# Routed results of a mixture of experts: through a buffer, or added to the stored output rows by the scatters

## The chip, the cores and the metric

The kernel runs on one core of one Trainium2 chip. The metric is the device time of one execution in microseconds, where less is better. The profile is one execution recorded by the hardware profiler; its span runs from the first to the last instruction on the core, and its times are counted from the start of that span. Engines are called PE (matrix products; its weight loads have rows of their own, PEld), DVE (vector engine), ACT (scalar engine), POOL or GpSimd, and SP, which here only issues DMAs. The DMAs that move rows to places given by an index tensor ("indirect") are issued by GpSimd.

## The reference

One layer of three parts over 512 tokens (8 sequences of 64) of width 512, all in float32: three rounds of slot attention over contexts of 1601 rows, a self-attention with 16 heads, and a mixture of experts. Each part normalises its input and adds its result to x. Only the third matters here:

```python
logits = xf @ router_w + router_b                      # 512 tokens x 8 experts
topk_vals, topk_idx = jax.lax.top_k(logits, 2)
gates = softmax over the two chosen, 0 elsewhere
expert(x, w1, w3, w2) = (silu(x @ w1) * (x @ w3)) @ w2  # 512 -> 256 -> 512
routed_out = sum over the 8 experts of gate * expert(xf)
shared_out = expert_s0(xf) + expert_s1(xf)              # two experts that every token passes
return x + routed_out + shared_out
```

So each output row is the sum of the row of x, two shared results and two routed results.

## The kernel before, in words

The first two parts, and the norm in front of the third, fill the span up to about 844 us and are untouched. `xall` (line 125) holds the 512 rows of x as four tiles of 128 rows in on-chip memory; every part adds its result into it.

The third part goes as follows.

- *Routing* (lines 973 to 1055). DVE finds each token's two experts and gates. Rows that go to the same expert are packed into blocks of 128 rows; an expert's last block is padded. There are at least 8 and at most `NB` = 15 blocks; `NB_MOST` = 12 are always computed, the other three only under a condition (line 1147) that this run does not meet.
- *Rows out to the blocks* (lines 1057 to 1066). Eight indirect DMAs write each token's normalised row twice into `xbuf` in device memory, at its place in its block. A row in `xbuf` is `DX` = 514 wide: 512 values, then the row number to which its result goes (column `D`, an integer), then its gate (column `D + 1`). `xbuf` was first filled with zero rows whose row number is one past the last legal one (lines 899 to 905), so that padding rows are skipped by the bounds check of the later scatter. In the old kernel the row number is a place in `back`, which has one row for each token and choice: 1024 rows.
- *Shared experts*. `shared_up(e, tp, ...)` (line 850) computes the first two products and the gate of shared expert `e` for the token pair-tile `tp` (256 tokens); `shared_down` (line 868) does the last product, 8 matmuls in the trace's counting (rows `py_s`, line 875), and adds it into `xall` on DVE (line 880). There are four such combinations. (0,0) runs during the routing, (0,1) in front of the blocks. For (1,0) and (1,1) only `shared_up` runs in front of the blocks; their `shared_down` is kept in the list `later`.
- *Blocks*. `block_up(n)` (line 1084) issues on GpSimd's queue the load of the block's 128 rows from `xbuf` into an `xb` buffer (six of them), reads the block's expert number into a register on SP, and loads that expert's weights on SP's queue (`up_b`, `dn_b`; `up_b` has five buffers, tag `ctxT`). PE transposes the rows (`tr_xb`), DVE or ACT copies them out, PE multiplies (`pab`), ACT and DVE apply the gate function (`th`, `g`). `block_down(n)` (line 1102) transposes `g`, does the second product (`py`), ACT scales it by the gates into `y` (three buffers, line 1114), and GpSimd scatters the 128 rows of `y` with an indirect DMA (line 1115), taking the row numbers straight from `xb`. Program order is up of block n+1, then down of block n. The scatters are declared independent of each other (line 1122) because they write distinct rows.
- *The end* (lines 1149 to 1166). The two late `shared_down` run, and for each of the four row tiles `back`'s two results for a token are loaded by SP behind all scatters, added to `xall` (by DVE alone, or after GpSimd has added the two), and stored to `out` by a DMA on ACT's queue.

`queue` (line 127) issues a DMA on SP in the written order; `behind(inst, those)` (line 1068) makes an instruction wait for others. What is not tied by such a call or by `keep_in_program_order` may be placed by the scheduler in an order of its own within an engine's queue; each engine then works through its queue strictly in order, so an instruction that waits holds up all behind it.

Of the kernel before, what the change touches and what calls it, by code (L numbers as in the profile page):

```python
# [9 lines left out]
F32 = mybir.dt.float32  # L10
I32 = mybir.dt.int32
AF = mybir.ActivationFunctionType
ALU = mybir.AluOpType
AX = mybir.AxisListType

P = 128
D = 512
DC = D // P
B, S = 8, 64
NPAIR = B * S // P  # L20
# [7 lines left out]
TOP = 2  # L28
DX = D + 2
NB_MOST = 12  # L30
# [10 lines left out]
def perceiver_kernel(  # L41
# [7 lines left out]
    nc = tc.nc  # L49
# [5 lines left out]
    dram = ctx.enter_context(  # L55
        tc.tile_pool(name="dram", bufs=1, space=bass.MemoryType.DRAM)
    )
# [10 lines left out]
    def chunk(name, tag="w"):  # L68

        bufs, width = SLOTS[tag]  # L70
        return big.tile([P, width], F32, tag=tag, name=name, bufs=bufs)
# [4 lines left out]
    def bank(name, tag="ring"):  # L76
        return ps.tile([P, 512], F32, tag=tag, name=name)
# [47 lines left out]
    xall = const.tile([P, NPAIR, D], F32, name="xall")  # L125

    def queue(dst, src):

        return tc.keep_in_program_order(nc.sync.dma_start(dst, src))  # L129
# [32 lines left out]
    def matmul4(dst, lhsT, rhs, start=True, stop=True):  # L162
        for c in range(DC):
            last = nc.tensor.matmul(  # L164
                dst, lhsT=lhsT(c), rhs=rhs(c),
                start=start and c == 0, stop=stop and c == DC - 1,
            )
        return last
# [55 lines left out]
    places, tag_of = [], {}  # L224
# [306 lines left out]
    def recur_more(t, banks, c):  # L531

        for j, k in ((2, DC - 1), (1, c))[c > 0 :]:
            tc.keep_in_program_order(nc.tensor.matmul(  # L534
                banks[j], lhsT=sT_of[t][:, k, :], rhs=whh_s[j][:, k, :],
                start=k == 0, stop=j == 2,
            ))
# [109 lines left out]
    for pos, (half, (t, it)) in enumerate(stages[:-1]):  # L647
# [21 lines left out]
        if it == 0:  # L669
# [14 lines left out]
            t, it, fill=lambda c: recur_more(other[0], begun[other], c)  # L684
# [159 lines left out]
    def gated(dst, th, pa, pb):  # L844

        nc.scalar.activation(th, pa, AF.Tanh, scale=0.5)
        nc.vector.scalar_tensor_tensor(th, th, 1.0, pa, ALU.add, ALU.mult)
        nc.vector.scalar_tensor_tensor(dst, th, 0.5, pb, ALU.mult, ALU.mult)

    def shared_up(e, tp, tags):  # L850

        up = shared[e][0]
        n = f"s{e}_{tp}"
        cols = ts(tp, 2 * P)
        g = chunk(f"g_{n}", tags[1])[:, :D] if tags[1] in SLOTS else work.tile(
            [P, D], F32, tag=tags[1], name=f"g_{n}", bufs=3
        )
        g = g.rearrange("p (c m) -> p c m", c=HC)
        for hc in range(HC):
            pab = bank(f"pab_{n}_{hc}")  # L860
            pa, pb = pab[:, : 2 * P], pab[:, 2 * P :]
            matmul4(pa, lambda c: up[:, c, ts(hc, P)], lambda c: hT[:, c, cols])
            matmul4(pb, lambda c: up[:, c, ts(HC + hc, P)], lambda c: hT[:, c, cols])
            th = work.tile([P, D], F32, tag=tags[0], name=f"th_{n}_{hc}")[:, : 2 * P]
            gated(g[:, hc, :], th, pa, pb)
        return g

    def shared_down(e, tp, g, at=lambda add: add()):

        dn = shared[e][1]  # L870
        for h in range(2):
            t = 2 * tp + h
            py = bank(f"py_s{e}_{tp}_{h}")
            for hc in range(HC):
                nc.tensor.matmul(  # L875
                    py, lhsT=g[:, hc, ts(h, P)], rhs=dn[:, hc, :],
                    start=hc == 0, stop=hc == HC - 1,
                )
            at(lambda t=t, py=py: tc.keep_in_program_order(
                nc.vector.tensor_add(xall[:, t, :], py, xall[:, t, :])  # L880
            ))
# [13 lines left out]


    xbuf = dram.tile([NB * P, DX], F32, name="xbuf")
    back = dram.tile([TOP * NPAIR * P, D], F32, name="back")
    zeros = chunk("zeros")[:, :DX]
    nc.gpsimd.memset(zeros, 0.0)  # L900
    nc.gpsimd.memset(zeros[:, D : D + 1].bitcast(I32), TOP * NPAIR * P)
    tc.keep_in_program_order(nc.gpsimd.dma_start(
        xbuf.rearrange("(b p) d -> p b d", p=P),
        zeros.unsqueeze(1).to_broadcast([P, NB, DX]),
# [3 lines left out]
    for i in range(TOP):  # L908
        rows = chunk(f"rows_{i}")[:, : NPAIR * DX].rearrange("p (t d) -> p t d", d=DX)
        nc.gpsimd.iota(  # L910
            rows[:, :, D].bitcast(I32), pattern=[[P, NPAIR]], base=i * NPAIR * P,
            channel_multiplier=1,
        )
        rows_of.append(rows)
# [8 lines left out]
    def part_of(*shape):  # L923
        n = shape[0] * shape[-1] if len(shape) > 1 else shape[0]
        lo = taken[0]
        taken[0] += n
        v = room[:, lo : lo + n]
        return v.rearrange("p (t e) -> p t e", e=shape[-1]) if len(shape) > 1 else v

    before, every, numbers = part_of(P), part_of(P), part_of(NB)  # L930
    rank, base = part_of(NPAIR, E), part_of(NPAIR, E)
# [4 lines left out]
        out=before, in_=before, compare_op=ALU.is_ge, fill=0.0, base=-1,  # L936
        pattern=[[1, P]], channel_multiplier=-1,
# [72 lines left out]
    blocks = sums[0][:, E:]  # L1010
# [46 lines left out]
    for t in range(NPAIR):  # L1057
        for i in range(TOP):
            at = bass.IndirectOffsetOnAxis(ap=place[i][:, t : t + 1], axis=0)
            s = nc.gpsimd.indirect_dma_start(  # L1060
                out=xbuf[:], out_offset=at, in_=rows_of[i][:, t, :], in_offset=None
            )
# [5 lines left out]
    def behind(inst, those, reason="rows of the blocks"):  # L1068
        for s in those:
            tc.add_manual_dep(  # L1070
                inst.ins, s.ins.name,
                mybir.DependencyInfo(
                    mybir.DependencyClass.Sync, mybir.DependencyReason.DATA
                ),
                reason=reason,
            )
# [25 lines left out]
    def block_down(n, xb, g, dn):  # L1102
        pt = bank(f"tr_g_{n}")[:, :HF].rearrange("p (c m) -> p c m", c=HC)
        for c in range(HC):
            nc.tensor.transpose(pt[:, c, :], g[:, ts(c, P)], ident)
        gT = work.tile([P, HC, P], F32, tag="gT", name=f"gT_{n}", bufs=2)
        nc.vector.tensor_copy(gT, pt)
        py = bank(f"py_{n}", "gate")
        for c in range(HC):
            nc.tensor.matmul(  # L1110
                py, lhsT=gT[:, c, :], rhs=dn[:, c, :], start=c == 0, stop=c == HC - 1
            )
        y = work.tile([P, D], F32, tag="y", name=f"y_{n}", bufs=3)
        nc.scalar.mul(y, py, xb[:, D + 1 :])
        s = nc.gpsimd.indirect_dma_start(
            out=back[:], in_=y, in_offset=None,
            out_offset=bass.IndirectOffsetOnAxis(ap=xb[:, D : D + 1].bitcast(I32), axis=0),
            bounds_check=TOP * NPAIR * P - 1, oob_is_err=False,
        )
        if n < NB_MOST:  # L1120
            if returned:
                tc.declare_no_dep(s.ins, group="returned", reason="rows of distinct places")
            tc.add_to_no_dep_group("returned", s.ins)
            returned.append(s)

    returned = []
    later = []
    for e, tp in ((0, 1), (1, 0), (1, 1)):
        later.append((e, tp, shared_up(e, tp, ("th", "g"))))
        if e == 0:  # L1130
            shared_down(*later.pop())

    def run_blocks(lo, hi):
        up_next = block_up(lo)
        for n in range(lo, hi):
            now = up_next
            if n + 1 < hi:
                up_next = block_up(n + 1)
            block_down(n, *now)
# [6 lines left out]

    with tc.If(total > NB_MOST):
        run_blocks(NB_MOST, NB)
    for part in later:
        shared_down(*part)  # L1150
    for t in (1, 0, 3, 2):
        y2 = chunk(f"back_{t}", "ctxT")[:, : TOP * D].rearrange("p (i d) -> p i d", i=TOP)
        behind(
            queue(y2, back.rearrange("(i t p) d -> p t i d", t=NPAIR, p=P)[:, t]),
            returned, "results of the blocks",
        )
        parts = [y2[:, 0, :]]
        if t % 2:
            parts.append(y2[:, 1, :])
        else:  # L1160
            nc.gpsimd.tensor_add(y2[:, 0, :], y2[:, 0, :], y2[:, 1, :])  # L1161
        for y in parts:
            tc.keep_in_program_order(
                nc.vector.tensor_add(xall[:, t, :], xall[:, t, :], y)  # L1164
            )
        nc.scalar.dma_start(out[ts(t, P), :], xall[:, t, :])


# [40 lines left out]
```

## Time and profile before

| | us |
|---|---|
| median of 3 runs (lowest, highest) | 971.46 (969.67, 978.85) |
| the profiled execution | 971.95 |
| its span | 970.1 |
| busy in the span: PE, DVE, ACT, POOL | 924.9, 417.8, 242.2, 199.5 |
| everything ahead of the packed rows | 0 to 854 |
| eight scatters of rows into `xbuf` | first at 854.5, last at 863.5 |
| six first loads of `xb` issued | from 869.2 |
| first and last product row of the blocks on PE | 877.2 to 952.6 |
| scatters of results (line 1115), 12 | first at 888.0, last at 953.6 |
| stores of the output (line 1166), 4 | first at 962.1, last at 967.1 |

How to read the views: a row has the line of the kernel, the engine, the operation, and the tiles "out<-in". In the timeline the first number is the start, the second the length, and brackets hold the idle time of the engine before the row with what ended it; a releaser is inferred, and where several things were waited for it names one of them. "POOL ... DMA_INDIRECT" is the time in which GpSimd makes the transfer's descriptors, not the transfer. The time from issue to landing is given by the views of one tile. For the tile `back` it reads:

```profile
L1115 POOL DMA_INDIRECT back<-y,xb x12: 984/1022/1032, 888.0 to 953.6; - x12
DMA to landing us min/median/max: 2.3/3.4/6.1
```

The three numbers are minimum, median and maximum: of the instruction's length in ns in the first line, of the time to landing in us in the second.

### The profile page before, as it was taken

How to read it: one execution, taken by the hardware profiler on the slowest of the kernel's cores; microseconds unless marked ns; L12 is line 12 of the kernel's file. 1: busy time of each engine (PE TensorE's matmuls, PEld its weight loads, DVE VectorE, ACT ScalarE, POOL GpSimd, SP SyncE). 2: the span in 40 equal slices, each digit the busy share in tenths (PEclk: the TensorE clock that was granted, in tenths of full speed). 3: DMA queues.
4: the chain of work that ended last, by engine and by line, in shares of the span. 5: the costliest groups of instructions: out<-in, count | busy, mean ns of one | idle time of the engine just before them, and what ended most of it. 6: DMA issues, size and time to landing. Idle time of an engine off the chain costs nothing. (4 is left out here: it accounts for less than half of the span.)

```text
span 970.1 us, 11778 instructions
## 1 busy us (share of the span) xinstructions
PE 924.9 (95%) x4081; PEld 439.9 (45%) x4081; DVE 417.8 (43%) x1111; ACT 242.2 (25%) x594; POOL 199.5 (21%) x319
## 2 busy tenths in 40 slices
PE   6999989999999999999999999999999887998995
PEld 2546444443444445455443434344443455584442
DVE  2216544262625356554453635353531637432223
ACT  1357541111111127446211111111200123101220
POOL 2012422030302023312211203030332110041212
PEclk9999999999999999999999999999999999899998
DMA  9997598393939397969947767585834200059934
GB/s 333 350 376 296 219 393 343 110 409 115 394 115 399 122 362 253 373 204 353 396 191 266 276 237 305 211 331 188 301 131 143 74 1 1 1 196 367 370 130 152
DMA packets 85852, 237.45 MB, mean 245 GB/s; under 512 B 8558, under 2 KB 24958, under 8 KB 85792
## 3 DMA queue, kind: packets, MB, share of 16 engines
q1 hardware_dynamic: 73312, 195.45, 55.0%
q0 software_dynamic: 11328, 39.14, 10.6%
q10 hardware_dynamic: 1152, 2.10, 0.6%
q8 instruction: 33, 0.54, 0.2%
q14 instruction: 27, 0.22, 0.1%
HBM read 201.22 MB, written 36.48 MB: 245 GB/s over the span
## 5 line engine op out<-in xcount | busy, mean ns | idle before, releaser
L504 POOL TENSOR_TENSOR raw<-e,rms 128x512 f32<-128x512 f32 (+1 forms) x48 | 45.6, 960 | 406.4 <-DVE e L502 375.1
L460 PE MATMUL sc<-ring_ctxT,qT 128*64 128x512 f32 x296 | 97.6, 599 | 1.2 <-DVE qT L444 0.8
L549 PE MATMUL pu<-ring_nat,e 128*64 128x512 f32 x308 | 94.5, 596 | 0.0
L460 PE MATMUL sc<-ring_nat,qT 128*64 128x512 f32 x280 | 91.3, 594 | 0.0
L549 PE MATMUL pu<-ring_ctxT,e 128*64 128x512 f32 x268 | 86.0, 596 | 0.0
L495 DVE TENSOR_REDUCE mx<-tr_e 128x8 f32<-128x512 f32 (+1 forms) x48 | 26.8, 585 | 102.0 <-PE tr_e L483 101.6
L468 ACT ACTIVATE raw<-sc,sri 128x512 f32<-128x512 f32 (+1 forms) x48 | 27.4, 595 | 100.8 <-PE sc L460 100.8
L460 PEld LDWEIGHTS sc<-ring_ctxT,qT 128*64 128x64 f32 x296 | 28.5, 137 | 49.2 <-issue 42.5
L164 PE MATMUL pwvi<-wih,wv 128*128 128x512 f32 x96 | 44.9, 614 | 4.3 <-ACT wqk L412 4.3
L534 PE MATMUL pz<-whh,sT 128*128 128x512 f32 x96 | 48.0, 594 | 0.0
L164 PE MATMUL pab<-up_b,xT 128*128 128x512 f32 x96 | 43.2, 594 | 0.8 <-ACT xT L87 0.7
L525 PE MATMUL pr<-whh,sT 128*128 128x512 f32 x96 | 43.9, 594 | 0.0
L164 PE MATMUL pqkv<-wqkv,haT 128*128 128x512 f32 x96 | 42.2, 596 | 1.4 <-ACT haT L713 1.4
L164 PE MATMUL pq<-wqk,sT 128*128 128x512 f32 x96 | 43.5, 595 | 0.0
L549 PEld LDWEIGHTS pu<-ring_ctxT,e 128*64 128x64 f32 x268 | 24.9, 137 | 40.9 <-issue 39.3
L164 PE MATMUL pr<-wvi,uT 128*128 128x512 f32 x96 | 43.3, 593 | 0.0
L164 PE MATMUL pz<-wvi,uT 128*128 128x512 f32 x96 | 43.2, 592 | 0.0
L164 PE MATMUL pxn<-wvi,uT 128*128 128x512 f32 x96 | 43.2, 592 | 0.0
L460 PEld LDWEIGHTS sc<-ring_nat,qT 128*64 128x64 f32 x280 | 27.6, 137 | 32.6 <-issue 29.9
L549 PEld LDWEIGHTS pu<-ring_nat,e 128*64 128x64 f32 x308 | 27.7, 137 | 30.4 <-issue 28.9
L365 DVE COPY ring_ctxT<-tr_p 128x256 f32<-128x256 f32 x60 | 24.0, 419 | 38.7 <-PE tr_p L111 25.0
L368 ACT ACTIVATE ring_nat<-ring_nat 128x512 f32<-128x512 f32 x54 | 34.5, 640 | 14.5 <-PE tr_p L111 11.3
(259 smaller groups left out, 1453.9 us busy)
## 6 DMA issues: line engine op xcount, KB each, us to landing
ring_nat<-in_ctxp SPq DMA_DIRECT2D x104, 512.0 KB
ring_ctxT<-in_ctxp SPq DMA_DIRECT2D x88, 512.0 KB
ring_ctxT<-kept SPq DMA_DIRECT2D x48, 512.0 KB
ring_nat<-kept SPq DMA_DIRECT2D x48, 512.0 KB
kept<-ring_ctxT POOLq DMA_DIRECT2D x26, 512.0 KB, 5.9
up_b<-in_w SPq DMA_DIRECT2D x24, 512.0 KB
kept<-ring_nat POOLq DMA_DIRECT2D x22, 512.0 KB, 8.3
dn_b<-in_w SPq DMA_DIRECT2D x12, 512.0 KB
```

The costliest lines, as they stand in the source:

```text
L164: last = nc.tensor.matmul(dst, lhsT=lhsT(c), rhs=rhs(c), start=start and c == 0, stop=stop and c == DC - 1,)
L365: nc.vector.tensor_copy(parts[0][:, :, cols], pt[:, :2, :])
L368: nc.scalar.activation(src, src, AF.Square, accum_out=ss[:k, i, j : j + 1])
L460: nc.tensor.matmul(sc[j * S : (j + 1) * S, :], lhsT=qT[:, c, ts(j, S)], rhs=cols, start=c == 0, stop=c == DC - 1,)
L468: nc.scalar.mul(raw[:, lo:hi], sc, ri)
L495: nc.vector.reduce_max(mxr, rows3(pt), axis=AX.X)
L504: nc.gpsimd.tensor_mul(rows3(prod), ee, wide(rms))
L525: nc.tensor.matmul(banks[j], lhsT=sT_of[t][:, c, :], rhs=whh_s[j][:, c, :], start=c == 0, stop=False,)
L534: tc.keep_in_program_order(nc.tensor.matmul(banks[j], lhsT=sT_of[t][:, k, :], rhs=whh_s[j][:, k, :], start=k == 0, stop=j == 2,))
L549: nc.tensor.matmul(pu[j * S : (j + 1) * S, :], lhsT=e[:k, i, ts(j, S)], rhs=row_tile("Y", t, it, j, i), start=i == 0, stop=i == MT,)
```

## The change

The buffer `back` goes. The row number that travels with each row is now the token's own (0 to 511, padding 512), and the scatters of line 1115 write to `out` itself, with an addition: each row of `y` is added to the row that is stored there. As two blocks may add to the same token's row, each scatter is made to wait until the one ahead of it has landed; the first waits for the four stores that put `xall` into `out`. So that these stores hold x and all shared results, the `shared_down` of all combinations run in front of the blocks, and the stores follow them there, on ACT's queue. The loads of `back`, the additions on DVE and GpSimd and the stores at the end are removed.

```diff
-    back = dram.tile([TOP * NPAIR * P, D], F32, name="back")
-    nc.gpsimd.memset(zeros[:, D : D + 1].bitcast(I32), TOP * NPAIR * P)
+    nc.gpsimd.memset(zeros[:, D : D + 1].bitcast(I32), NPAIR * P)
...
-            rows[:, :, D].bitcast(I32), pattern=[[P, NPAIR]], base=i * NPAIR * P,
+            rows[:, :, D].bitcast(I32), pattern=[[P, NPAIR]], base=0,
...
         s = nc.gpsimd.indirect_dma_start(
-            out=back[:], in_=y, in_offset=None,
+            out=out, in_=y, in_offset=None, compute_op=ALU.add,
             out_offset=bass.IndirectOffsetOnAxis(ap=xb[:, D : D + 1].bitcast(I32), axis=0),
-            bounds_check=TOP * NPAIR * P - 1, oob_is_err=False,
+            bounds_check=NPAIR * P - 1, oob_is_err=False,
         )
-        if n < NB_MOST:
-            if returned:
-                tc.declare_no_dep(s.ins, group="returned", reason="rows of distinct places")
-            tc.add_to_no_dep_group("returned", s.ins)
-            returned.append(s)
-
-    returned = []
-    later = []
+        behind(s, written, "rows of the output")
+        written[:] = [s]
+
     for e, tp in ((0, 1), (1, 0), (1, 1)):
-        later.append((e, tp, shared_up(e, tp, ("th", "g"))))
-        if e == 0:
-            shared_down(*later.pop())
+        shared_down(e, tp, shared_up(e, tp, ("th", "g")))
+    written = [nc.scalar.dma_start(out[ts(t, P), :], xall[:, t, :]) for t in range(NPAIR)]
...
     with tc.If(total > NB_MOST):
         run_blocks(NB_MOST, NB)
-    for part in later:
-        shared_down(*part)
-    for t in (1, 0, 3, 2):
-        y2 = chunk(f"back_{t}", "ctxT")[:, : TOP * D].rearrange("p (i d) -> p i d", i=TOP)
-        behind(
-            queue(y2, back.rearrange("(i t p) d -> p t i d", t=NPAIR, p=P)[:, t]),
-            returned, "results of the blocks",
-        )
-        parts = [y2[:, 0, :]]
-        if t % 2:
-            parts.append(y2[:, 1, :])
-        else:
-            nc.gpsimd.tensor_add(y2[:, 0, :], y2[:, 0, :], y2[:, 1, :])
-        for y in parts:
-            tc.keep_in_program_order(
-                nc.vector.tensor_add(xall[:, t, :], xall[:, t, :], y)
-            )
-        nc.scalar.dma_start(out[ts(t, P), :], xall[:, t, :])
```

## The prediction

> **What bounds the kernel now.** I read the page first, then the stretches of the last stage, the chain of waits, PE, and GpSimd's own timeline. Over the span PE is busy 95%, but the change lies behind 854 us, so that stage decides. The table of stretches (columns: stretch, length, busy time of PE, PEld, DVE, ACT, POOL with counts, granted clock, DMA share, GB/s):
>
> ```profile
> 854.00:874.20 20.20, 20.19 (x86) 15.91 (x84) 5.60 (x12) 1.57 (x5) 11.13 (x14) 1.00 0.74 254
> 874.20:877.20 3.00, 1.26 (x8) 0.85 (x9) 1.44 (x3) 0.42 (x2) 0.00 (x0) 1.00 1.05 397
> 877.20:930.00 52.80, 51.06 (x150) 24.41 (x151) 12.40 (x30) 11.12 (x21) 10.58 (x13) 1.00 1.04 358
> 930.00:952.90 22.90, 21.36 (x61) 9.63 (x59) 4.57 (x12) 4.71 (x9) 3.98 (x4) 1.00 0.11 43
> 952.90:970.10 17.20, 7.10 (x16) 2.92 (x16) 6.73 (x10) 0.47 (x1) 3.64 (x3) 0.82 0.53 192
> ```
>
> PE sets the pace of the blocks (about 6.15 us each: block products start at 931.24, 937.39 and 943.56). DMA is full until 930 and then nearly idle. Behind 952.9 PE has only the 7.1 us of late shared sums. The chain of waits shows what ends the kernel, the trip of the results through memory:
>
> ```profile
> 952.89 3.69 PE py_s L875 x8
> ...
> 957.68 5.50 DMA back<-back
> 963.18 1.63 issue
> ...
> 966.38 0.69 DVE xall L1164
> ```
>
> GpSimd's timeline is the view that matters most (start, length, what; in brackets the idle time before it and its releaser):
>
> ```profile
> 888.05 1.03 POOL L1115 DMA_INDIRECT back<-y,xb  x1 [15.53 <-ACT y L1114]
> 894.64 0.56 POOL L1087 DMA_DIRECT2D xb<-xbuf  x1 [5.56 <-DMA back<-y,xb]
> 895.51 1.03 POOL L1115 DMA_INDIRECT back<-y,xb  x1 [0.30 <-issue]
> 902.29 0.56 POOL L1087 DMA_DIRECT2D xb<-xbuf  x1 [5.75 <-PE py L1110]
> 903.15 1.03 POOL L1115 DMA_INDIRECT back<-y,xb  x1 [0.30 <-ACT y L1114]
> 904.49 1.01 POOL L1115 DMA_INDIRECT back<-y,xb  x1 [0.31 <-issue]
> ...
> 913.98 1.02 POOL L1115 DMA_INDIRECT back<-y,xb  x1 [1.80 <-ACT y L1114]
> 920.19 0.57 POOL L1087 DMA_DIRECT2D xb<-xbuf  x1 [5.19 <-issue]
> 921.07 1.03 POOL L1115 DMA_INDIRECT back<-y,xb  x1 [0.30 <-issue]
> 928.09 0.56 POOL L1087 DMA_DIRECT2D xb<-xbuf  x1 [5.99 <-issue]
> 928.95 1.03 POOL L1115 DMA_INDIRECT back<-y,xb  x1 [0.30 <-issue]
> ...
> 953.64 0.98 POOL L1115 DMA_INDIRECT back<-y,xb  x1 [1.74 <-ACTq L1147]
> ```
>
> The reader is to see that scatters already stand one behind another here, by accident. There are six xb buffers; the seventh load waits until the first scatter, which reads its row numbers from the first buffer, has landed, and the next scatter is queued behind that load. Call the scatters s0 to s11. Four links are of this form: 888.05 to 895.51, to 903.15, and 913.98 to 921.07, to 928.95, that is 7.46, 7.64, 7.09, 7.88, mean 7.5 us. So with DMA full, a plain chain runs slower than PE (6.15). Landings, counted from the issue: 6.1 (s0) and 5.7 (s4) with DMA full; 2.6, 3.4 and 2.3 (s9, s10, s11) when it is idle.
>
> **The change, part by part.** Sums are against the profiled execution: span 970.1, 971.95 in all, so 1.85 lie around the span; the median of the three runs shown is 0.5 below it.
>
> *Shared sums moved forward.* The 16 matmuls of L875 (7.1 us, from 952.89) go in front of the blocks. PE's cover there is the stretch 874.2 to 877.2, where 3.00 − 1.26 = 1.7 us are idle waiting for xb loads; without it the price is 7.1. The last g is ready only at 876.2, so part of the idle time may stay. I take 1.3 as covered: the blocks start 5.8 us later (bounds 5.3 and 7.1). DVE's four adds (0.69 each) move too and find DVE idle. Four output stores go on ACT's queue in front of the blocks, about 0.35 each, behind the last add; what queues behind them is the first block's th, due at 880.92 + 5.8 = 886.7, while the stores are issued by about 884: covered. They carry 1 MB, 2.9 us at 358 GB/s, into the full stage, and s0 waits for all four; s0 is due at 888.05 + 5.8 = 893.9, so 10 us are there for a landing that took at most 8.0 for any xb load.
>
> *Removed at the end.* SP's four loads of back (issued over 1.93), six DVE adds, two GpSimd adds and the late stores: all that lies between 954.62 and the end. s11 is instead followed by its own landing and the end of the program. Behind the last store's issue (967.06 to 967.4) the old span has 2.7 us, landing included; I take 0.7 behind a landing (0 to 2.7).
>
> *If the chain costs nothing*: s11 at 953.64 + 5.8 = 959.4, landing 2.3 to 3.4, and 0.7: span 962.4 to 963.5, or 964.3 to 965.4 in all, 0.7% below. That is the most the change can give unless idle time inside the blocks closes too.
>
> *The chain.* Now every scatter waits for its predecessor's landing. Queued behind the waiting scatter on GpSimd are the xb loads of later blocks; ACT waits for the y buffers (three) three blocks later. The order within the queue I take as before (xb loads behind s0, s1, two behind s3, one each behind s4, s5).
>
> *The addition.* No accumulating scatter is in this trace. Lower bound 0: the read of the output rows overlaps the rest. Upper bound: it is a whole read in front of the write, like an xb load (5.2 us at least). Below nothing is excluded: it moves the same bytes and more. Nearest rows: the landings of scatters with DMA idle differ by 3.4 − 2.3 = 1.1 us, with the number of rows that are in range, which prices moving a block's rows once more. I take 1.1 quiet, 1.5 with DMA full. A link is then 7.5 + 1.5 = 9.0 with an xb load in it, 8.15 without (0.86 less); quiet 3.4 + 1.1 + 0.5 for the reaction (the load at 894.64, 0.5 behind s0's landing) = 5.0, or 5.9 with an xb load. DMA is full to about 932, since the weights follow the blocks' later buffers.
>
> s0 893.9, s1 902.9, s2 911.9, s3 920.1, s4 929.9 (two loads between); then quiet: s5 935.8, s6 941.7, s7 946.7, s8 951.7, s9 956.7, s10 961.7, s11 966.7. It lands at 971.2; span 971.9; with 1.85, 973.8; less the 0.5 of the median, **973**. Does PE stall? y of block 7 is due at 932.2 + 5.8 = 938.0, s4 has landed at 934.4: no. The xb load of block 9 is issued at 928.3, lands about 934.4, due 934.5: just. So the chain, 7 us late at the end, eats what the shorter tail gives. One microsecond more or less per landing moves the end by 12 us, down to the floor above.
>
> The Trainium skill ("DMA: Bandwidth & Descriptors", section on the anatomy of a SWDGE DMA) prices a DMA from GpSimd at 2.0 us plus bytes over 436 GB/s, which is an estimate of 2.6 us for a block. The trace agrees when DMA is idle (2.3 to 3.4) and shows more than double when it is full (5.7 to 6.1); by the page no link would exceed 6.15, and the sum would be the floor, about 965. "Collectives: The Full Stack" (section on the bandwidth ceiling) says that an add in the DMA path costs through its two source reads and not through the arithmetic; as an estimate 0.6 us more per block, and again about 965. No run here shows it yet.
>
> **Rivals.** *The chain binds throughout* (slower): the addition costs a link 3 us instead of 1.1 to 1.5, because read and write follow one another. Then 12 × 1.6 = 19 us more, 993. It decides from where the addition exceeds about 2 us: 0.65 us more per link are 8 us, 981. For it: links of 7.1 to 7.9 already exceed PE's pace, and xb loads for blocks 9 and on have no slack left. Against: DMA is idle from 932, where five or six links can catch up. Chance 0.42.
>
> *The chain stays hidden* (0.7% faster): the addition is nearly free, s4 comes at 924, and the quiet links of 3.9 catch up with PE by s8. For it: the four accidental links cost the old kernel no PE stall. Against: the first four links are over 6.15. Chance 0.24; 0.05 of it for over 1%, if some of the 3.3 us of PE's idle time within the blocks closes too.
>
> *The wait is not new*, so that only the tail changes: excluded as a whole, since s2 to s3 (903.15, 904.49) and s6 to s7 did overlap.
>
> **How the numbers follow.** The forecast (late chain, caught up in part, 965.5 to 981) has 0.34, the hidden chain 0.24, the binding chain 0.42. About 1% is what a measurement of this kernel tells from no change: 961.7 to 981.2. Faster 0.05, within 0.53, slower 0.42. The range starts at 963.5, below the floor's 964.3, and reaches to 996, just over the rival's 993; beyond it lies an addition of over 3 us, 0.15. The likeliest case's own range is 965.5 to 981.
>
> **What would show it.** GpSimd's timeline: scatters spaced about 9 us until 930 and about 5 behind it, s11 near 967 while its y is there at 959. Spacing near 6.15 to the end, set by y, means the hidden chain; spacing over 6.5 after 935 the binding one. PE's first block product at 883 shows the shift; PE waiting for xb in blocks 8 to 11, or ACT's y waiting for a DMA, would show a stall that I priced at nothing. I am wrong at the root if landings with DMA full shorten because PE-paced weight loads leave gaps.

## The result, and the profile after

The changed kernel takes 981.65 us (median of 4 runs, 980.18 to 987.73) against 971.47 for the kernel before: a ratio of 1.010, interval 1.0066 to 1.0134. The profiled execution took 980.94, its span is 979.2, 9.1 us over the old one. The forecast was 973, a change within 1%. The measurement lies 0.5 us past the line that the prediction drew at 981.2, so by the number it belongs to the case "slower", which had a chance of 0.42 against 0.53; by the mechanism it lies between the two, as is shown below.

The chain of waits ends in scatters now, not in loads and additions:

```profile
968.80 4.60 DMA out<-y,xb
...
974.18 1.54 POOL out L1115
```

The table of stretches, over the products of the first two blocks with PE's idle time between them, the rest of the time with DMA full, the time behind it, and the time behind PE's last product (columns as before the change):

```profile
883.10:893.30 10.20, 6.97 (x12) 2.95 (x13) 0.84 (x2) 0.87 (x2) 0.00 (x0) 0.83 1.08 367
893.30:930.00 36.70, 35.19 (x106) 16.78 (x105) 8.84 (x21) 7.43 (x14) 8.20 (x7) 1.00 1.00 314
930.00:964.70 34.70, 32.09 (x93) 14.80 (x91) 7.39 (x18) 7.90 (x14) 10.76 (x9) 1.00 0.39 97
964.70:979.20 14.50, 0.00 (x0) 0.00 (x0) 0.00 (x0) 0.00 (x0) 3.65 (x3) 0.63 0.28 36
```

The first row is new: PE works 7.0 of 10.2 us there, at a granted clock of 0.83. GpSimd's timeline:

```profile
899.08 1.65 POOL L1115 DMA_INDIRECT out<-y,xb  x1 [26.01 <-ACT y L1113]
906.58 0.58 POOL L1086 DMA_DIRECT2D xb<-xbuf  x1 [5.86 <-DMA out<-y,xb]
907.47 1.59 POOL L1115 DMA_INDIRECT out<-y,xb  x1 [0.30 <-issue]
...
933.01 1.66 POOL L1115 DMA_INDIRECT out<-y,xb  x1 [0.49 <-issue]
...
941.27 1.62 POOL L1115 DMA_INDIRECT out<-y,xb  x1 [1.19 <-ACT xT L87]
...
957.26 1.56 POOL L1115 DMA_INDIRECT out<-y,xb  x1 [3.84 <-issue]
963.71 1.55 POOL L1115 DMA_INDIRECT out<-y,xb  x1 [4.89 <-issue]
...
974.18 1.54 POOL L1115 DMA_INDIRECT out<-y,xb  x1 [3.84 <-DMA out<-y,xb]
```

The first scatter comes at 899.08 instead of the forecast 893.9. From it to the last there are eleven links in 75.1 us, 6.8 each, where PE delivers a y about every 6.15. The last y is ready at 964.66 (its row on ACT starts at 963.97 and takes 0.69); the last scatter leaves 9.5 us later. The view of the tile `out`, to compare with that of `back`:

```profile
L1115 POOL DMA_INDIRECT out<-y,xb x12: 1544/1594/1662, 899.1 to 974.2; - x12
...
DMA to landing us min/median/max: 3.6/4.7/8.2
```

An adding scatter holds GpSimd 1.6 us where a plain one held it 1.0. It lands 1.3 us later at the minimum and the median and 2.1 later at the maximum (2.3/3.4/6.1 before). The landing is counted from the start of GpSimd's row, so the 0.6 by which that row is longer lies within these differences; whether the rest is the read of the stored rows isn't shown.

Executions differ by some microseconds ahead of the last stage already, with the number of short stretches at half the granted clock (mean clock 0.977 to 0.989 in the profiled executions). So stages are compared below from the issue of the six first xb loads, which is 869.23 before and 869.78 after:

| from the profile, us | before | after |
|---|---|---|
| six loads to the first scatter | 18.8 | 29.3 |
| first to last scatter | 65.6 | 75.1 |
| last scatter to the end | 16.5 | 5.0 |
| sum | 100.9 | 109.4 |

The end got shorter by 11.5, as the change wants it. The other two terms, 10.5 and 9.5, are what has to be explained.

### The profile page after: what moved, and what is told of

It is laid out like the page before. It is cut to its first block, busy times and chain, and to the rows that moved or that the text cites. A ratio compares the mean times of both kernels' runs of the same rounds, so it can differ in the third digit from the quotient of the medians.

```text
span 979.2 us, 11749 instructions
## 1 busy us (share of the span) xinstructions
PE 926.1 (95%) x4081; PEld 439.8 (45%) x4081; DVE 414.1 (42%) x1105; ACT 241.6 (25%) x594; POOL 203.5 (21%) x317
## 3 DMA queue, kind: packets, MB, share of 16 engines
q0 software_dynamic: 12096, 39.15, 11.5%
## 5 line engine op out<-in xcount | busy, mean ns | idle before, releaser
L460 PEld LDWEIGHTS sc<-ring_nat,qT 128*64 128x64 f32 x280 | 27.6, 137 | 32.6 <-issue 29.8
L549 PEld LDWEIGHTS pu<-ring_nat,e 128*64 128x64 f32 x308 | 27.7, 137 | 30.5 <-issue 28.6
```

The costliest lines, as they stand in the source:

```text
L460: nc.tensor.matmul(sc[j * S : (j + 1) * S, :], lhsT=qT[:, c, ts(j, S)], rhs=cols, start=c == 0, stop=c == DC - 1,)
L549: nc.tensor.matmul(pu[j * S : (j + 1) * S, :], lhsT=e[:k, i, ts(j, S)], rhs=row_tile("Y", t, it, j, i), start=i == 0, stop=i == MT,)
```

## The experiments

Each ratio is to the kernel before as it was measured together with the run. Theory A, from the trace after: the first term is the moved sums (about 5) and a block on ACT's queue (about 5.5); the second is the addition together with the chain of waits, which neither causes alone. The rivals are named with each run.

**Who holds the first scatter?** ACT's timeline after the change:

```profile
881.67 7.67 ACTq L1125 DMA_DIRECT2D out<-xall  x2
889.39 0.58 ACT L87 COPY xT<-tr_xb 128x512 f32<-128x512 f32 x1 [10.63 <-DMA up_b<-in_w]
889.87 0.39 ACT L846 ACTIVATE th<-pab 128x256 f32<-128x256 f32 x1
```

and PE's:

```profile
883.15 3.70 PE L164 MATMUL pab<-up_b,xT 128*128 128x512 f32 x8 [0.51 <-DVE xT L85]
890.03 5.33 PE L164 MATMUL pab<-up_b,xT 128*128 128x512 f32 x8 [3.17 <-ACT xT L87]
```

Two stores are issued between 881.67 and 889.34, though a store takes ACT only 0.34 us and the last addition was done at 882.5. Behind the second stands block 1's copy to xT, and PE waits 3.17 us for it; then eight matmuls take 5.33 instead of 3.60, the clock of 0.83 in the table above. The program's list of instructions for ACT says what the fourth store waits for (number, line, what, waits):

```
452 L1125 DMACopy out<-xall_74 128x512 [waits DMAHW3_49,DVE_49]
453 L1125 DMACopy out<-xall_74 128x512 [waits DMAHW4_49,DVE_49]
454 L87 TensorCopy xT_1_5556<-tr_xb_1_5557 128x512 [waits PE_49]
```

In this program the DMAs of SP and ACT take eight completion semaphores (0 to 7) in turn; number 4 had been given to the first weight load of block 3, issued by SP at 878.36. The fourth store waits for the semaphore to come free, so for a load that has nothing to do with it and needs until about 889, some 10.6 us, with DMA full. ACT's row above names the same releaser: its copy waited 10.63 us, to the end of a load of `up_b`. SP's row of the two loads is

```profile
878.36 2.76 SPq L129 DMA_DIRECT2D up_b<-in_w  x2
```

The run that undoes this:

```diff
-    written = [nc.scalar.dma_start(out[ts(t, P), :], xall[:, t, :]) for t in range(NPAIR)]
+    written = [nc.gpsimd.dma_start(out[ts(t, P), :], xall[:, t, :]) for t in range(NPAIR)]
```

> The changed kernel, with the four early output stores issued by GpSimd instead of ACT. Theory A (the fourth store holds ACT's queue until 889.0, because it waits for an unrelated weight load; block 1's copy stands behind it): PE's 3.2 us stall and the slow clock behind it go, the first scatter comes at about 894 instead of 899.1, the links of the chain stay as they are, so the span falls by about 5 us to 974 (976 in all; 975 to 978). Rival (the chain's pace is set by when the weight loads end, not by when it starts): the first scatter comes earlier, the last one does not: 979 to 982.

Measured: 977.99, ratio 1.0069 (1.0041 to 1.0096). PE's first two products run through,

```profile
883.73 7.13 PE L164 MATMUL pab<-up_b,xT 128*128 128x512 f32 x16 [0.51 <-DVE xT L85]
...
894.59 1.65 POOL L1115 DMA_INDIRECT out<-y,xb  x1 [10.68 <-ACT y L1113]
...
970.27 1.54 POOL L1115 DMA_INDIRECT out<-y,xb  x1 [3.87 <-issue]
```

without the slow clock, and the first scatter comes 23.75 behind the loads (870.84 here), 5.5 earlier. The last one comes 99.4 behind them instead of 104.4, so 5.0 of the 5.5 reach the end of the chain. The eleven links take 75.7 instead of 75.1: the first four are longer (37.6 in place of 33.9; their scatters land after 7.3 to 8.3 us in place of 5.9 to 8.2), the fifth is shorter (4.8 in place of 8.3). The reason isn't shown. The medians differ by 3.7; this profiled execution was itself 1.1 later at the loads. The block on ACT's queue is shown; the rival has a small share.

**The moved sums alone**, in the kernel before (`shared_down` follows `shared_up` at once, so the `later` list stays empty):

```diff
-        later.append((e, tp, shared_up(e, tp, ("th", "g"))))
-        if e == 0:
-            shared_down(*later.pop())
+        shared_down(e, tp, shared_up(e, tp, ("th", "g")))
```

> The kernel before with only the shared sums moved in front of the blocks; back, plain and free scatters and the old end stay. Theory A (the move shifts the blocks by 5.8 us on PE, and nothing of the old end gets shorter by it): last scatter at 959.4, span 975 to 977, 977 to 979 in all. Rival (the shared sums fit in idle time in front, or the end shortens by them): 971 to 973.

Measured: 980.36, ratio 1.0074 (1.0046 to 1.0101). First scatter 23.95 behind the loads (5.1 later), 65.6 to the last, 16.7 to the end: the shift goes through to the end whole, and nothing of the old end shrinks. By themselves the moved sums cost about what the prediction put down, in time that was free behind the last block; 5.1 us are 0.5%, at the lower end of the interval.

**Addition and chain, each alone and both**, in the kernel before with its old end. For the addition, `back` is filled with zeros by a DMA issued behind that of `xbuf` and the scatter gets `compute_op=ALU.add`; what the fill costs by itself was not measured. For the chain:

```diff
-        if n < NB_MOST:
-            if returned:
-                tc.declare_no_dep(s.ins, group="returned", reason="rows of distinct places")
-            tc.add_to_no_dep_group("returned", s.ins)
-            returned.append(s)
+        behind(s, returned[-1:])
+        if n < NB_MOST:
+            returned.append(s)
```

> The kernel before with adding scatters into a back that is filled with zeros earlier; no chain of waits. Theory A (the addition costs only through the landing that something waits for): the last landing is 1.3 us later, 972 to 974 in all. Rival (the addition itself slows the weight loads or GpSimd enough to hold the blocks up): 978 or more.

> The kernel before with plain scatters that wait one for another. Theory A (a plain chain falls behind PE only while DMA is full, and quiet links of about 4 us catch up): the last scatter at 953.6 to 955, 971 to 973 in all. Rival (a chain costs what it costs, addition or not): last scatter at 960 or later, 978 or more.

> The kernel before, its shared sums and its end as they were, but the scatters into back add (back is filled with zeros earlier) and wait one for another. Theory A (chain and addition together make the last scatter late, whatever stands in front of the blocks): first scatter at 888, eleven links as in the changed kernel (75 us), last one at 963, then the old end of 16.5 us and 1.3 more for the landing: span 979 to 982, 981 to 984 in all. Rival (the loss is in what was moved in front of the blocks, not in the chain): 971 to 974.

| | median, us | ratio to before (interval) | first to last scatter, us |
|---|---|---|---|
| addition alone | 973.92 | 1.0021 (1.0004 to 1.0038) | 65.6 |
| chain alone | 974.57 | 1.0029 (1.0006 to 1.0052) | 67.3 |
| both | 984.56 | 1.0121 (1.0094 to 1.0147) | 76.6 |

The single effects add up to 0.5%; together they cost 1.2%, and the gap is wider than the intervals. That is theory A's mark. Scatters that are free to overlap hide a longer landing (65.6 us with the addition and without). A plain chain catches up with PE once DMA is idle and loses 1.7 us, all of it at the last scatter, whose y comes only 2.7 us after the one ahead. With the addition inside the chain both parts grow. The first four links, with DMA full, take 38.9 us instead of the plain chain's 29.8, which is 2.3 more a link. Behind that a link is only a little shorter than PE's 6.15, so the chain can't make up what it lost: in the changed kernel the scatter at 941.27 leaves 10.4 us behind its y, the one at 968.80 still 6.9.

```profile
930.19 0.69 ACT L1113 ACTIVATE y<-py,xb 128x512 f32<-128x512 f32 x1 [1.53 <-PE py L1109]
...
961.25 0.69 ACT L1113 ACTIVATE y<-py,xb 128x512 f32<-128x512 f32 x1 [2.39 <-PE py L1109]
```

PE was hit too, in the last of the three:

```profile
930.17 0.63 PE L111 MATMUL tr_xb<-ident,xb 128*128 128x128 f32 x4 [2.67 <-DMA xb<-xbuf]
```

Block 8's rows came late because their load is queued behind scatters that wait (in the changed kernel the same wait is 0.42). The slow clock followed here too: the twelve matmuls of 128x512 behind this row take 1.6 us longer than elsewhere, and the granted clock from 930 to 934 is 0.67. So part of this run's cost is PE's.

**The chain without the addition, in the changed kernel:**

```diff
-            out=out, in_=y, in_offset=None, compute_op=ALU.add,
+            out=out, in_=y, in_offset=None,
```

> The changed kernel with the addition left out of the scatters: each writes its rows over what is stored, so the routed and shared results are not summed; the chain of waits stays. Theory A (the addition lengthens each landing by 1 to 1.5 us and thereby makes the chain slower than PE): links of about 7.5 us with DMA full and 4 when it is idle, the chain catches up with y before the end, the last scatter comes at 965, span 968 to 969, 970 to 971 in all. Rival (the waits alone cost it, the addition is nearly free): 977 or more.

Measured: 974.01, ratio 1.0000 (0.9969 to 1.0031). Eleven links take 67.3, as in the plain chain above, so the rival falls. It misses theory A's number by 3 us: in the profiled execution the first scatter comes 30.5 behind the loads, 1.2 more than in the changed kernel, and the last scatter still waits for its predecessor's landing:

```profile
970.37 0.98 POOL L1115 DMA_INDIRECT out<-y,xb  x1 [3.40 <-DMA out<-y,xb]
```

This run and the changed kernel allow a comparison of the same scatters (counted from s0), behind the time of full DMA:

| landing, us from issue | s6 | s7 | s8 | s9 | s10 | s11 |
|---|---|---|---|---|---|---|
| without the addition | 2.4 | 2.6 | 2.7 | 2.6 | 3.6 | 2.3 |
| with it | 3.6 | 4.7 | 4.7 | 4.3 | 4.6 | 3.6 |

The addition costs 1.0 to 2.1 us a landing there, 1.6 in the mean, which is more than the difference of 1.3 between the medians of all twelve.

**The loads between the links.** The stores on GpSimd as above, and `keep_in_program_order` on scatters and xb loads, written so that the load for block n + 5 is issued just behind the scatter of block n (the first six ahead of the shared experts):

```diff
             block_down(n, *now)
+            if 1 <= n and n + 5 < NB_MOST:
+                load_xb(n + 5)
```

> The changed kernel with the early stores on GpSimd, and GpSimd's queue in a written order in which the load of a later block's rows stands behind the next scatter instead of in front of it. Theory A (a load between landing and next scatter lengthens a link by 0.87): six such terms go, 5 us more than the stores alone; last scatter at 962 to 965, 969 to 973 in all, about level with the kernel before. Rival (the links are set by the landings, the loads between them fit in): as with the stores alone.

Measured: 973.49, ratio 1.0002 (0.9982 to 1.0022). First to last scatter 72.6 instead of 75.7: 3.1 us of the 5.2 that six loads of 0.87 would give. It is level with the kernel before.

**Fewer weight loads in flight.** The load that took 10.6 us to land suggests that a scatter stands behind a heap of loads of 512 KB. In the written-order kernel each of the blocks' 36 weight loads now waits for the one two, three or four ahead of it:

```diff
+    def pace(inst):
+        if len(paced) >= 3:
+            tc.add_manual_dep(
+                inst.ins, paced[-3].ins.name,
...
+        paced.append(inst)
```

> The kernel with the written order on GpSimd (a_ordered), and each of the 36 weight loads of the blocks waits until the load two ahead of it has landed, so that two are in flight. Theory A (a scatter lands late with DMA full because several loads of 512 KB stand ahead of it): landings until 930 fall from 7 to 10 us to 5 to 6, links to about 6, the chain keeps close to PE, last scatter at 963 to 966: 966 to 970 in all. Rival (a landing is long because the bandwidth is shared, however few loads are queued): landings stay at 7 us or more, 973 or more. Third way (two in flight don't fill the DMA engines, the weights come late): PE waits for up_b, 976 or more.

> As a_paced2 with three weight loads in flight. Theory A: between a_ordered and a_paced2, 967 to 971. Rival: as a_ordered, 973. Third way: less of PE's wait than in a_paced2.

> As a_paced3 with four weight loads in flight. Theory A (fewer loads ahead of a scatter shorten its landing; fewer than three in flight make the weights late): between a_paced3 and a_ordered, landings with DMA full of 6 to 8 us, 971 to 974 against 973 for the kernel before. If four suffice to shorten the landings and end the weight loads sooner: 968 to 971.

> a_paced3 once more, to narrow its interval against the kernel before: theory A 2 us below it (ratio 0.997 to 0.999); if the first measurement was chance: 1.000 or more.

| in flight | median, us | ratio to before (interval) | first to last scatter, us |
|---|---|---|---|
| two | 974.67 | 1.0026 (1.0005 to 1.0047) | 75.1 |
| three | 971.50 | 0.9984 (0.9963 to 1.0005) | 69.6 |
| three, again | 970.86 | 0.9978 (0.9959 to 0.9996) | 68.3 |
| four | 973.84 | 1.0012 (0.9990 to 1.0033) | 73.2 |

In the written order alone the third and the fourth scatter land after 7.4 and 7.6 us; with three loads in flight they land after 5.7 and 6.7, in the repetition after 6.0 and 6.7. With two, landings are 5.0 to 6.8 until 930, but PE stalls, as the third way said, though at 974.67 and not at 976 or more. PE's row in front of the last block's products shows it; it names SP's queue, which had issued the second load of this block's `up_b` only at 952.12:

```profile
959.00 5.29 PE L164 MATMUL pab<-up_b,xT 128*128 128x512 f32 x8 [3.20 <-SPq L1170]
```

Three in flight is the one version here that was measured below both kernels, by 0.2% against the one before; its first interval just includes no difference, its second does not. A limit on the loads in the kernel before was not tried, so it is open whether the change has any part in this gain. The end of its GpSimd timeline:

```profile
959.28 1.56 POOL L1140 DMA_INDIRECT out<-y,xb  x1 [3.66 <-issue]
964.67 1.55 POOL L1140 DMA_INDIRECT out<-y,xb  x1 [3.83 <-issue]
```

Of the eleven runs, four came out within theory A's numbers (the stores on GpSimd, the addition alone, four in flight, three again). Six took 0.5 to 3 us longer than theory A's upper number, and two in flight took 4.7 longer.

## Why the prediction was right or wrong

Its mechanism held: a late chain, caught up only in part, eats what the shorter end gives. Its size did not: the shorter end gave 11.5, the later start took 10.5 and the chain 9.5, where the forecast had 11.3, 5.8 and 7.2. The forecast span was 7.3 us short, and by its own terms that splits as follows.

- *Shift of the blocks, 5.8*: nearly right, a little too dear. 4.9 to 5.1 where ACT's queue was free (the stores on GpSimd, the moved sums alone), below the bounds of 5.3 to 7.1; PE's first block product came at 883.15 against 883 forecast.
- *"Covered" stores on ACT's queue, 0*: wrong, and the largest miss. I counted four issues of 0.35 and took block 0's `th` for the instruction behind them. Block 1's copy to xT stood there, and a store's issue itself can wait for a DMA of SP. With DMA full that wait ran to 889, and the first scatter came 5.2 later than forecast; 1.7 of it is the slow clock that followed PE's idle time.
- *Links with DMA full, 36.0 for four*: 33.9, with single links of 8.4, 9.1, 8.9 and 7.4. Too dear here, but not because 1.5 for the addition was enough: in the pair of plain and adding chain it costs 2.3 a link, and with the stores on GpSimd the same four links take 37.6. In the changed kernel the weight loads, which follow the late blocks, leave some gaps (DMA share 0.83 from 915 to 925).
- *Links behind it, 36.8 for seven*: 41.2. DMA was still busy (share 0.78) from 932 to 938, where the forecast had it idle from 932, and the fifth link was 8.3 instead of 5.9: its landing took 6.0, and 1.2 us in front of the scatter at 941.27 are put down to a copy of ACT that the scatter has no need of. The link of 957.26 to 963.71 is 1.5 longer than forecast. Its scatter leaves 1.7 behind its predecessor's landing at 962.0, and the profile names no cause. It isn't the chain alone: in the kernel before the same scatter leaves 1.5 behind its y (ready at 944.50), the one ahead of it 0.3.

```profile
943.81 0.69 ACT L1114 ACTIVATE y<-py,xb 128x512 f32<-128x512 f32 x1 [1.54 <-PE py L1110]
...
946.01 0.99 POOL L1115 DMA_INDIRECT back<-y,xb  x1 [6.42 <-issue]
```

- *A quiet link, 5.0*: 4.4, 5.4, 5.1 and 5.4 in the others without a load, so right, but with luck. The base of 3.4 was the longest quiet landing of the kernel before (most plain landings in the table above took 2.3 to 2.7), the addition's 1.1 was too small, and the two errors cancel. That the 1.1 prices moving a block's rows once more was argued from the number of rows; no run shows it.
- *Landing and end, 5.2*: 5.0.
- *PE stalls, 0*: besides the one on ACT's queue 0.42 us, at block 8; the load for which I had found no slack was block 9's.

So 5.2 of the 7.3 are the start of the chain and 2.3 its links, less 0.2 at the end. At the last scatter the chain is 9.5 us behind its y, where 7 were forecast.

Of the rivals, "the chain binds" is the case into which the time falls, by 0.5 us, but its price was too high: the addition costs 1.0 to 2.1 a landing with DMA idle and 2.3 a link with DMA full, not 3. That the chain stays behind PE to the end doesn't tell it from the forecast, which says so too. Its own sign, a spacing over 6.5 behind 935, did not come: the six links from 941.27 on take 5.5 in the mean. The hidden chain is excluded by the pair of addition and chain above.

What the Trainium skill's two pages gave, a sum of 965, failed. "DMA: Bandwidth & Descriptors" (anatomy of a SWDGE DMA) gives 2.6 by its formula, which fits an idle DMA, 2.3 to 3.4 plain. With DMA full a plain scatter took 5.7 to 6.1 in the kernel before and an adding one up to 8.2 in the changed one, and there the measurement decides. The second source read, which I priced at 0.6 after "Collectives: The Full Stack" (the bandwidth ceiling), stands against the 1.0 to 2.1 that the whole addition cost, of which 0.6 are GpSimd's longer row.

## What to carry to other kernels

A chain of dependent DMAs has a period of its own: landing, reaction and whatever is queued between two of them. Compare it with the period of the engine that feeds it, for full and idle DMA separately; a longer landing that overlap would hide becomes time at the end as soon as the links are tied, and free time behind the last block is the cheapest place for independent work. Before putting a DMA on a compute engine's queue, look in the program's waits for what its issue needs besides its data.

## What the runs showed of the hardware

With a limit of three weight loads in flight the third and fourth scatter landed after 5.7 to 6.7 instead of 7.4 and 7.6 us, and PE was not starved; with two PE waited 3.20 us in front of the last block.

An idle PE was followed by the half clock: 3.17 us of it cost 1.7 us on the next eight matmuls in the changed kernel, and 2.67 us cost 1.6 on the next twelve in the run with addition and chain; after 1.57 us, with the stores on GpSimd, the clock stayed at 1.0. "TensorE: Matmul & The Clock Gate" (section on why this matters for your kernels) sets the gap to avoid at about 3 us. The first of these rows agrees; the second shows that less can be enough, and the measurement decides.
